# First pass of a two-layer attention kernel: turns and checks moved into the next step, products of qkv placed elsewhere in the step

## The chip, the cores and the metric

The kernel runs on one core of a Trainium2 chip. The metric is the device time of one execution in microseconds (us). Three runs of the kernel before gave a median of 4059.47 us (4054.06 to 4061.17). One execution was taken by the hardware profiler; it took 4056.18 us, with a span of 4054.4 us from the first to the last instruction. TensorE's granted clock was 0.992 over it.

The profile names the engines PE (TensorE matmul), PEld (TensorE's weight loads), DVE (VectorE), ACT (ScalarE), POOL (GpSimd) and SP (SyncE, which issues the DMAs here). L774 is line 774 of the kernel. An f32 matmul of 128x512 shows as two records, so "x8" in a row of the timeline is four matmuls.

## The reference

Two layers on an image batch of shape (8, 256, 64, 64), all in f32. Only layer 0 and the first product of layer 1 matter here; the rest is named.

```python
# layer 0: attention whose keys and values come from a 4x4 strided convolution
xr = conv(x, w_sr, stride 4); xr = layernorm over channels(xr) * g + b      # 16x16 places
q = w_q @ x;  k, v = split(w_kv @ xr)                                       # 8 heads of 32
attn = softmax(q k^T / sqrt(32))                                            # 4096 x 256 per head
x = x + gamma_s * (w_out @ (attn v))
# layer 1
qkv = w_qkv @ x                                                             # 768 x 4096 per image
agg = grouped 1x1 of depthwise 5x5 of qkv
x = x + batchnorm(w_proj @ relu_linear_attention(concat(qkv, agg)))
```

## The kernel before, in words

There are three passes, one after the other. The first does layer 0 and the product qkv of layer 1, and leaves its results in DRAM scratch (`planes`, `kd`, `vd`, `x2d`). The second does the convolution and the sums of layer 1, the third its output. Then a flag `fine`, made from checks in the first pass, says whether a general version must run instead; it does not run with these inputs. Only `first_pass` is touched.

**The loop of the first pass.** Its unit is a step n, one element of `order`: image b (8), strip s of 512 pixels (8), half c of the heads (2), half kc of the keys (2), so 256 steps, and some more at the end for what is left. A step n with kc = 1 is odd. In each step the code asks for, in this order:

- `scores` (L774): four matmuls, one head each, in four strips of 32 rows of TensorE, each into a bank of its own; then four Exp on ScalarE (L780) into tiles `e`.
- `valued` of the step before (L791): four matmuls into the tile `av`, in four strips of 32 columns.
- after both halves of the keys: `counted` (L807), the softmax sums `den`, from tiles `e` that `joined` (L802) has added on GpSimd; and `normed`, which divides. `normed` turns `den` on VectorE (L817), takes reciprocals of 16 columns (L818), turns them back (L820) and multiplies (L822). Two ScalarE activations of 128x512 (L823, L824) add up `den` and the reciprocals into `seen`, for the flag.
- `queries` (L759), the next q, in even steps.
- the work that `todo` holds for this step: `outputs` (`added`, L831 and L832: the product o with `w_out`, added to x, stored by L835), `differences` (L847 to L850), and products of `qkv`. The code asks for these last in the step, just ahead of the next step's scores.
- in some steps of an image, pieces of the next image's `keys_values` (sr at L687, mean, var, rs, k, v).

**The product qkv.** `w_qkv @ x` is done for a pair of row blocks and two strips by seven products in place of eight (`p1`, `p2`, `p6`, `p7`, `p4`, `p5`, `p3`). The sums of differences `t1` to `t4` and of weights `s1` to `s4` stand in for the eighth. Each product is one matmul of 128x512 (L875) into a bank; p1 is copied out by ScalarE (L925), the others are added on VectorE to an earlier part: L932, L936, L945 for the intermediate parts, `ended` for the outputs. For the outputs of pair 0, `ended` adds straight into a padded tile `stage` (L888). For pairs 1 and 2 it adds into `part_whole` (L891) and turns that with VectorE's 32x32 transpose into `turned` (L894); for pair 1 ScalarE also copies it into `stage` (L893). `stored` sends `stage` (L902) and `turned` (L912 for keys, L917 for values) to DRAM through SP's queue. `new_stage` clears two edges of a stage tile on GpSimd (L855, L856). A unit is done for every two strips, so in a cycle of 8 steps there are 21 products.

**Buffers.** `bank` gives one of five PSUM banks, tag "mm", to scores, q, o, qkv and the small products of the keys; a bank is used again when its reader is done. `av`, `den` and `sr` have banks of their own. `part_whole` has two buffers, each `stage` of pairs 0 and 1 one of its own (four tags), the tiles `e` twelve.

**What sets the order.** A scheduler builds each engine's stream from the code's order and the data. It can move instructions that are ready early. `tc.keep_in_program_order` pins an instruction behind all that its engine has been given so far. Each engine then takes its own stream in order; SP's DMA issues are one such stream.

Of the kernel before, what the change touches and what calls it, by code (L numbers as in the profile page):

```python
# [27 lines left out]
F32 = mybir.dt.float32  # L28
AF = mybir.ActivationFunctionType
ALU = mybir.AluOpType  # L30
AX = mybir.AxisListType

P = 128
# [541 lines left out]
def first_pass(ctx: ExitStack, tc: tile.TileContext, a, fine, planes, x2d, kd, vd, wtd):  # L575
# [207 lines left out]

    sums = {}

    def valued(b, s, c, kc, es):
        if kc == 0:
            sums["av"] = psum_early.tile([P, QB], F32, tag="av", name=f"av_{b}_{s}_{c}")
        for h in range(4):
            cols = slice(h * D0, (h + 1) * D0)  # L790
            nc.tensor.matmul(  # L791
                sums["av"][cols],
                vvs[b][:, kc, c * P + h * D0 : c * P + (h + 1) * D0],
                es[h],
                start=(kc == 0),
                stop=(kc == 1),
            )
# [11 lines left out]
    def normed(b, s, c):  # L809
        av, den = sums["av"], sums["den"]  # L810
        i = 2 * ((b * NG + s) * 2 + c)
        att = rest.tile([P, QB], F32, tag="att", name=f"att_{b}_{s}_{c}", bufs=4)
        r = rest.tile([P, NB, D0], F32, tag="rden", name=f"rden_{b}_{s}_{c}", bufs=1)
        one = two.tile([P, NB], F32, tag="one", name=f"one_{b}_{s}_{c}")
        nc.scalar.copy(att, av)

        nc.vector.transpose(r.rearrange("p n d -> p (n d)"), den)  # L817
        nc.vector.reciprocal(one, r[:, :, 0])  # L818
        r = rest.tile([P, NB, D0], F32, tag="rall", name=f"rall_{b}_{s}_{c}", bufs=1)
        nc.vector.transpose(r, one.unsqueeze(2).to_broadcast([P, NB, D0]))  # L820
        r = r.rearrange("p n d -> p (n d)")
        nc.vector.tensor_mul(att, att, r)  # L822
        nc.scalar.activation(den, den, AF.Copy, accum_out=seen[:, i : i + 1])  # L823
        nc.scalar.activation(den, r, AF.Copy, accum_out=seen[:, i + 1 : i + 2])  # L824
        return att

    def added(b, s, att, oc):
# [23 lines left out]
        quarters[b, g] = b11, b21, b22, t1, t2, t3, t4  # L851

    def new_stage(b, g, j):
        st = rest.tile([P, 4, NB + 1, NB + 1], F32, tag=f"stage{j}", name=f"stage_{b}_{g}_{j}", bufs=1)
        nc.gpsimd.memset(st[:, :, 0 if g // 2 else NB], 0.0)  # L855
        nc.gpsimd.memset(st[:, :, :, 0 if g % 2 else NB], 0.0)  # L856
        return st


    def qkv(b, g, pair):  # L860
        js = 2 * pair, 2 * pair + 1
        b11, b21, b22, t1, t2, t3, t4 = quarters[b, g]
        w = consts["wqkv"].rearrange("p c (j r o) -> p c j r o", j=3, r=2)[:, :, pair]
        s1, s2, s3, s4 = (combined[:, pair, i] for i in range(4))
        name = f"{b}_{g}_{pair}"
        stages = [new_stage(b, g, j) for j in js] if pair < 2 else None
        turned = None
        if pair:
            turned = [
                rest.tile([P, NB // 2, 4, D0], F32, tag=f"turned{j}", name=f"turned_{b}_{g}_{j}", bufs=1) for j in js  # L870
            ]

        def product(i, w, x):
            ps = bank(f"qkv_{name}_{i}")
            nc.tensor.matmul(ps, w, x, start=True, stop=True)  # L875
            return ps

        def part(i, bufs=1):
            return halves.tile([P, QB], F32, tag=f"part{i}", name=f"part_{name}_{i}", bufs=bufs)


        def ended(r, h, u, ps, op=ALU.add):
            if stages:
                y, x = g // 2, g % 2
                inside = stages[r][:, 2 * h : 2 * h + 2, y : y + NB, x : x + NB]
            rows = lambda t: t.rearrange("p (f y x) -> p f y x", f=2, y=NB)
            if not turned:
                nc.vector.tensor_tensor(inside, rows(u), rows(ps), op)  # L888
                return
            whole = part("whole", 2)  # L890
            nc.vector.tensor_tensor(whole, u, ps, op)  # L891
            if stages:
                nc.scalar.copy(inside, rows(whole))  # L893
            nc.vector.transpose(  # L894
                turned[r][:, :, 2 * h : 2 * h + 2].rearrange("p y f e -> p f y e"),
                whole.rearrange("p (f y e) -> p f y e", f=2, y=NB // 2),
            )

        def stored(r):
            j = js[r]  # L900
            if stages:
                nc.sync.dma_start(  # L902
                    planes[b, j].rearrange("g (k i f) e -> g k i (f e)", k=4, i=D1)[:, g],
                    stages[r].rearrange("p f y x -> p (f y x)"),
                )
            if not turned:
                return
            for k in range(4):
                n, src = 4 * (j % 2) + k, turned[r][k * D0 : (k + 1) * D0].rearrange("p y f e -> p y (f e)")
                if j < 4:  # L910
                    dst = kd[b][n].rearrange("a (y w) x b e -> a b (w x) y e", w=2)
                    nc.sync.dma_start(dst[g // 2, g % 2], src)  # L912
                else:
                    dst = vd[b][n][1 : NB2 + 1, 1 : NB2 + 1]
                    dst = dst.rearrange("(y w a) (x b) e -> a b w x y e", w=2, a=2, b=2)
                    for w in range(2):
                        nc.sync.dma_start(dst[g // 2, g % 2, w], src[w * NB : (w + 1) * NB])  # L917


        u = {}  # L920

        def p1():
            ps = product(1, w[:, 0, 0], b11)
            u[1] = part(1)
            nc.scalar.copy(u[1], ps)  # L925

        def p2():
            ended(0, 0, u[1], product(2, w[:, 1, 0], b21))

        def p6():  # L930
            u[2] = part(2)
            nc.vector.tensor_add(u[2], u[1], product(6, s2, t2))  # L932

        def p7():
            u[3] = part(3)
            nc.vector.tensor_add(u[3], u[2], product(7, s3, t3))  # L936

        def p4():
            ended(1, 0, u[3], product(4, w[:, 1, 1], t4), ALU.subtract)

        def p5():
            ps = product(5, s1, t1)
            ended(1, 1, u[3], ps)
            u[4] = part(4)
            nc.vector.tensor_add(u[4], u[2], ps)  # L945
            stored(1)

        def p3():
            ended(0, 1, u[4], product(3, s4, b22))
            stored(0)  # L950

        return [p1, p2, p6, p7, p4, p5, p3]

# [16 lines left out]
    q, es, att = {0: first}, {}, {}  # L970
    ahead = iter(())

    def outputs(b, s):
        return [lambda oc=oc: added(b, s, [att[b, s, 0], att[b, s, 1]], oc) for oc in range(2)]

    def qkv_lazy(b, g, pair):
        made = []

# [9 lines left out]

    n_all = len(order)
    todo = {}  # L990
    for n in range(n_all + 14):
        m = n - 1
        if n < n_all:
            b, s, c, kc = order[n]
            es[n] = scores(b, s, c, kc, q[n // 2])
        if 0 <= m < n_all:
            valued(*order[m], es[m])
            if order[m][3] == 1:
                counted(*order[m][:3], es.pop(m - 1))
                es.pop(m)  # L1000
                att[order[m][:3]] = normed(*order[m][:3])
        if n < n_all and kc == 1:
            joined(es[n - 1], es[n])
        if n < n_all and kc == 0 and n + 2 < n_all:
            q.pop(n // 2 - 1, None)
            q[n // 2 + 1] = queries(*order[n + 2][:3])
        if n >= 6 and (n - 6) % 8 == 4 and (n - 6) // 4 < B * NG:

            b, s = (n - 6) // 4 // NG, (n - 6) // 4 % NG
            work = [outputs(b, s) + [lambda b=b, s=s: differences(b, s // 2)]]  # L1010
            products = [p for pair in (1, 2, 0) for p in qkv_lazy(b, s // 2, pair)]
            for i in (4, 3, 4, 0, 3, 4, 3):
                work.append(products[:i])
                products = products[i:]
            for i, w in enumerate(work):
                todo.setdefault(n + i, []).extend(w)
        elif n >= 6 and (n - 6) % 8 == 0 and (n - 6) // 4 < B * NG:
            todo.setdefault(n, []).extend(outputs((n - 6) // 4 // NG, (n - 6) // 4 % NG))
        next(weights, None)
        if n < n_all:  # L1020
            b, at = n // 32, n % 32
# [2 lines left out]
            if b + 1 < B:  # L1024
# [6 lines left out]
                    next(ahead)  # L1031
                elif at >= 20:
                    next(ahead, None)
        for f in todo.pop(n, ()):
            f()
    for _ in weights:
        pass

# [3 lines left out]
    total = bank("total")[:, :2]  # L1042
    nc.tensor.matmul(total, mean_w, both, start=True, stop=True)
    fits = const.tile([P, 4], F32, tag="fits", name="fits")
    nc.vector.tensor_scalar(fits[:, 0:1], total[:, 0:1], SUM_MAX / C, None, ALU.is_le)
    nc.vector.tensor_scalar(fits[:, 1:2], total[:, 1:2], INVERSE_MAX / C, None, ALU.is_le)
    nc.vector.tensor_mul(fits[:, 2:3], fits[:, 0:1], fits[:, 1:2])
    nc.vector.tensor_copy(fine, fits[:, 2:3])

# [674 lines left out]
```

## Time and profile before

| | |
|---|---|
| median of 3 runs | 4059.47 us (4054.06 to 4061.17) |
| the profiled execution | 4056.18 us, span 4054.4 us |
| TensorE matmul busy | 3982.1 us |
| VectorE busy | 2262.4 us |
| ScalarE busy | 1644.2 us |
| GpSimd busy | 1275.1 us |
| first scores, and end of the first pass on TensorE | 52.42 us and 2154.75 us |
| turns L894, mean of one | 0.706 us |
| sums of products L891, mean of one | 0.67 us |
| stage copies L893, mean of one | 0.62 us |
| checks L823 and L824, mean of one, with the read of the sum | 0.582 + 0.194 and 0.602 + 0.186 us |
| GpSimd sums L802, mean of one | 1.320 us |

How to read it: a busy time is the time in which an instruction of the engine was under way, and for TensorE this includes time in which one of several matmuls in flight waits for its bank. Start-to-start distances in the timeline show such waits better than lengths do, since matmuls overlap by about 0.15 us. A row of the waits has the waiting line, the line waited for, the total in us, the number of times and the longest.

### The profile page before, as it was taken

To read this page: it belongs to the slowest core of one execution; us is meant where nothing else is said; L and a number is where in the kernel's file an instruction comes from. 1 tells how busy PE (TensorE), PEld (TensorE's weight loads), DVE (VectorE), ACT (ScalarE), POOL (GpSimd) and SP (SyncE) were. 2 spreads that over 40 slices of the span, in tenths; PEclk is the share of its full clock that TensorE was granted. 3 is DMA by queue.
4 is the path that set the end of the run, shared out by engine and by line. 5 is a ranking of instruction groups with operands and counts; after the bars stand their busy time and mean duration, and the time that the engine had idled before them with its cause. 6 is when DMAs were issued, how large, how long until landed. Compare 5 with 4: busy or idle time off the path is not lost. (4 is left out here: it accounts for less than half of the span.)

```text
span 4054.4 us, 70276 instructions
## 1 busy us (share of the span) xinstructions
PE 3982.1 (98%) x27074; PEld 2318.8 (57%) x27074; DVE 2262.4 (56%) x3752; ACT 1644.2 (41%) x3473; POOL 1275.1 (31%) x1394
## 2 busy tenths in 40 slices
PE   8999999999999999999998999999999998999999
PEld 4443434434334344343336888888888886556655
DVE  2676465564654545546565566666666664444443
ACT  3345354453544544534552222222222223454444
POOL 2344233333342433323343334434444441000000
PEclk9999999999999999999999999999999999999999
DMA  7665435445354354543549878778778656767674
GB/s 237 191 187 161 120 92 144 100 95 155 91 145 101 97 136 106 135 108 99 141 99 247 243 224 234 219 225 233 219 221 234 206 169 172 232 199 232 196 235 137
DMA packets 569898, 691.37 MB, mean 171 GB/s; under 512 B 60113, under 2 KB 429265, under 8 KB 565329
## 3 DMA queue, kind: packets, MB, share of 16 engines
q1 hardware_dynamic: 569552, 686.78, 60.6%
q8 instruction: 215, 3.52, 0.4%
q14 instruction: 131, 1.07, 0.1%
HBM read 412.54 MB, written 274.10 MB: 169 GB/s over the span
## 5 line engine op out<-in xcount | busy, mean ns | idle before, releaser
L802 POOL TENSOR_TENSOR e<-e,e 128x512 f32<-128x512 f32 x512 | 659.6, 1320 | 933.6 <-PE av L791 918.6
L780 ACT ACTIVATE e<-sc 128x512 f32<-128x512 f32 x1024 | 532.7, 601 | 708.8 <-PE sc L774 708.6
L774 PE MATMUL sc<-q,kk 32*128 32x512 f32 x2048 | 418.2, 641 | 7.5 <-ACT e L780 3.6
L1180 PE MATMUL cv<-w,c 128*128 128x128 f32 x3072 | 385.8, 280 | 6.0 <-POOL c L1124 6.0
L1180 PEld LDWEIGHTS cv<-w,c 128*128 128x128 f32 x3072 | 359.9, 193 | 35.5 <-issue 28.8
L1547 DVE TENSOR_TENSOR y<-z,xs 128x256 f32<-128x256 f32 x256 | 143.7, 648 | 312.8 <-ACT z L1538 305.2
L1222 PE MATMUL sums<-vq,r 128*32 128x288 f32 x4096 | 307.4, 413 | 0.0
L891 DVE TENSOR_TENSOR part_whole<-part,qkv 128x512 f32<-128x512 f32 x256 | 170.7, 670 | 219.6 <-PE qkv L875 215.8
L774 PEld LDWEIGHTS sc<-q,kk 32*128 32x128 f32 x2048 | 130.0, 183 | 276.3 <-issue 138.3
L1196 ACT ACTIVATE r<-s 128x512 f32<-128x512 f32 x256 | 160.5, 627 | 294.0 <-DVE s L1195 290.9
L875 PE MATMUL qkv<-differences,combined 128*128 128x512 f32 x576 | 278.7, 593 | 0.8 <-DVE differences L848 0.8
L791 PE MATMUL av<-e,vv 128*32 128x512 f32 x2048 | 275.6, 608 | 0.0
L1538 ACT ACTIVATE z<-p,bn 128x256 f32<-128x256 f32 x256 | 133.7, 578 | 315.9 <-PE p L1529 208.7
L759 PE MATMUL q<-x,wq 128*128 128x512 f32 x512 | 254.4, 619 | 0.0
L1184 PE MATMUL cv<-c,w 128*128 128x128 f32 x2048 | 253.4, 278 | 0.0
L1529 PE MATMUL p<-att,wproj 128*128 128x512 f32 x512 | 249.5, 610 | 1.9 <-ACT att L1512 1.9
L1187 ACT COPY both<-cv 128x512 f32<-128x512 f32 x128 | 74.9, 585 | 432.4 <-PE cv L1180 374.1
L687 PE MATMUL sr<-x,wsr 128*128 128x256 f32 x1024 | 237.2, 386 | 11.5 <-DMA wsr<-in_w_sr_dram 11.5
L1529 PE MATMUL p<-agg,wproj 128*128 128x512 f32 x512 | 241.7, 595 | 0.0
L1184 PEld LDWEIGHTS cv<-c,w 128*128 128x128 f32 x2048 | 239.7, 192 | 0.0
L687 PEld LDWEIGHTS sr<-x,wsr 128*128 128x128 f32 x1024 | 193.3, 192 | 76.3 <-issue 32.8
L831 PE MATMUL o<-att,wout 128*128 128x512 f32 x512 | 231.9, 594 | 0.0
(143 smaller groups left out, 6201.7 us busy)
## 6 DMA issues: line engine op xcount, KB each, us to landing
vq<-v SPq DMA_DIRECT2D x256, 384.0 KB
planes<-stage SPq DMA_DIRECT2D x128, 578.0 KB
d<-planes SPq DMA_DIRECT2D x128, 578.0 KB
raw<-planes SPq DMA_DIRECT2D x128, 272.0 KB
x<-in_xp_dram SPq DMA_DIRECT2D x64, 512.0 KB
wsr<-in_w_sr_dram SPq DMA_DIRECT2D x128, 256.0 KB
x<-x SPq DMA_DIRECT2D x128, 256.0 KB
k<-turned SPq DMA_DIRECT2D x256, 128.0 KB
```

Source lines behind the costliest of these rows:

```text
L687: nc.tensor.matmul(ps[:, oc], w[:, ci, oc * P : (oc + 1) * P], xt[:, ci, f * NK : (f + 1) * NK], start=(f == ci == oc == 0), stop=(f == R ...
L759: nc.tensor.matmul(ps, consts["wq"][:, ci, c * P : (c + 1) * P], x_tiles[b][:, ci, s * QB : (s + 1) * QB], start=(ci == 0), stop=(ci == 1),)
L774: nc.tensor.matmul(scs[h], kks[b][rows, c, kc * P : (kc + 1) * P], qs[rows], start=True, stop=True)
L780: nc.scalar.activation(e, scs[h], AF.Exp, scale=D0**-0.5)
L791: nc.tensor.matmul(sums["av"][cols], vvs[b][:, kc, c * P + h * D0 : c * P + (h + 1) * D0], es[h], start=(kc == 0), stop=(kc == 1),)
L802: nc.gpsimd.tensor_tensor(es0[h], es0[h], es1[h], ALU.add)
L831: nc.tensor.matmul(ps, consts["wout"][:, c, oc * P : (oc + 1) * P], att[c], start=(c == 0), stop=(c == 1))
L875: nc.tensor.matmul(ps, w, x, start=True, stop=True)
L1180: nc.tensor.matmul(out, x, m, start=(da == 0), stop=(da == 1))
L1184: nc.tensor.matmul(out, m, x, start=(da == 0), stop=(da == 1))
L1222: nc.tensor.matmul(ps[h * D0 : (h + 1) * D0, : 36 * D1].rearrange("p (r n e) -> p r n e", r=3, e=D1), kt[:, par, h, 2 * r + c], vq[:, r : ...
L1529: nc.tensor.matmul(ps.rearrange("p (f q n) -> p f q n", f=4, q=4), wproj[:, j, oc * P : (oc + 1) * P], src, start=(j == 0), stop=(j == 3),)
```

## The change

There are five edits, all in `first_pass`.

1. A list `late` holds functions that are to run in the next step, right after that step's scores. `ended` puts its turn and its stage copy there (both pinned in program order), for pairs 1 and 2; `ready` puts `stored` of these pairs there. `part_whole` becomes `whole`, with six buffers.
2. `normed` no longer reads 128x512 twice for the checks. It puts `noted` into `late`: two ScalarE copies of 128x16, of the first column of each turned block and of the reciprocals, with the same sums into `seen`. The limits in the flag are divided by 32 to fit.
3. The step's order changes. In odd steps the qkv products of that step come right after scores, ahead of `valued`. In even steps they come after `valued` and ahead of `queries`. `queries` comes ahead of `counted` and `normed`.
4. `added` runs within the step, after `joined`, in every fourth step as before; the 21 products are spread as 2, 3, 4, 1, 4, 3, 4 over the seven steps after it, where it was 4, 3, 4, 0, 3, 4, 3.
5. `stage` of pairs 0 and 1 share their buffers (two tags in place of four).

```diff
     def normed(b, s, c):
...
-        nc.scalar.activation(den, den, AF.Copy, accum_out=seen[:, i : i + 1])
-        nc.scalar.activation(den, r, AF.Copy, accum_out=seen[:, i + 1 : i + 2])
+
+        def noted():
+            for k, t in enumerate((turn[:, :, 0], one)):
+                copy = two.tile([P, NB], F32, tag="copy", name=f"copy_{b}_{s}_{c}_{k}")
+                tc.keep_in_program_order(
+                    nc.scalar.activation(copy, t, AF.Copy, accum_out=seen[:, i + k : i + k + 1])
+                )
+
+        late.append(noted)
...
     def new_stage(b, g, j):
-        st = rest.tile([P, 4, NB + 1, NB + 1], F32, tag=f"stage{j}", name=f"stage_{b}_{g}_{j}", bufs=1)
+        st = rest.tile([P, 4, NB + 1, NB + 1], F32, tag=f"stage{j % 2}", name=f"stage_{b}_{g}_{j}", bufs=1)
...
         def ended(r, h, u, ps, op=ALU.add):
...
-            whole = part("whole", 2)
+            whole = halves.tile([P, QB], F32, tag="whole", name=f"whole_{name}_{r}_{h}", bufs=6)
             nc.vector.tensor_tensor(whole, u, ps, op)
-            if stages:
-                nc.scalar.copy(inside, rows(whole))
-            nc.vector.transpose(
-                turned[r][:, :, 2 * h : 2 * h + 2].rearrange("p y f e -> p f y e"),
-                whole.rearrange("p (f y e) -> p f y e", f=2, y=NB // 2),
-            )
+
+            def turn():
+                tc.keep_in_program_order(
+                    nc.vector.transpose(
+                        turned[r][:, :, 2 * h : 2 * h + 2].rearrange("p y f e -> p f y e"),
+                        whole.rearrange("p (f y e) -> p f y e", f=2, y=NB // 2),
+                    )
+                )
+                if stages:
+                    tc.keep_in_program_order(nc.scalar.copy(inside, rows(whole)))
+
+            late.append(turn)
...
+        def ready(r):
+            if turned:
+                late.append(lambda: stored(r))
+            else:
+                stored(r)
...
-    for n in range(n_all + 14):
+    for n in range(n_all + 16):
         m = n - 1
         if n < n_all:
             b, s, c, kc = order[n]
             es[n] = scores(b, s, c, kc, q[n // 2])
+        was, late[:] = list(late), []
+        for f in was:
+            f()
+
+
+        if n % 2:
+            for f in todo.pop(n, ()):
+                f()
         if 0 <= m < n_all:
             valued(*order[m], es[m])
-            if order[m][3] == 1:
-                counted(*order[m][:3], es.pop(m - 1))
-                es.pop(m)
-                att[order[m][:3]] = normed(*order[m][:3])
-        if n < n_all and kc == 1:
-            joined(es[n - 1], es[n])
+        for f in todo.pop(n, ()):
+            f()
         if n < n_all and kc == 0 and n + 2 < n_all:
             q.pop(n // 2 - 1, None)
             q[n // 2 + 1] = queries(*order[n + 2][:3])
-        if n >= 6 and (n - 6) % 8 == 4 and (n - 6) // 4 < B * NG:
-
+        if 0 <= m < n_all and order[m][3] == 1:
+            counted(*order[m][:3], es.pop(m - 1))
+            es.pop(m)
+            att[order[m][:3]] = normed(*order[m][:3])
+        if n < n_all and kc == 1:
+            joined(es[n - 1], es[n])
+        if n >= 6 and (n - 6) % 4 == 0 and (n - 6) // 4 < B * NG:
             b, s = (n - 6) // 4 // NG, (n - 6) // 4 % NG
-            work = [outputs(b, s) + [lambda b=b, s=s: differences(b, s // 2)]]
-            products = [p for pair in (1, 2, 0) for p in qkv_lazy(b, s // 2, pair)]
-            for i in (4, 3, 4, 0, 3, 4, 3):
-                work.append(products[:i])
-                products = products[i:]
-            for i, w in enumerate(work):
-                todo.setdefault(n + i, []).extend(w)
-        elif n >= 6 and (n - 6) % 8 == 0 and (n - 6) // 4 < B * NG:
-            todo.setdefault(n, []).extend(outputs((n - 6) // 4 // NG, (n - 6) // 4 % NG))
+            for oc in range(2):
+                added(b, s, [att[b, s, 0], att[b, s, 1]], oc)
+            if s % 2:
+                differences(b, s // 2)
+                products = [p for pair in (1, 2, 0) for p in qkv_lazy(b, s // 2, pair)]
+                for i, count in enumerate((2, 3, 4, 1, 4, 3, 4)):
+                    todo[n + 1 + i] = products[:count]
+                    products = products[count:]
...
-        for f in todo.pop(n, ()):
-            f()
...
-    nc.vector.tensor_scalar(fits[:, 0:1], total[:, 0:1], SUM_MAX / C, None, ALU.is_le)
-    nc.vector.tensor_scalar(fits[:, 1:2], total[:, 1:2], INVERSE_MAX / C, None, ALU.is_le)
+    nc.vector.tensor_scalar(fits[:, 0:1], total[:, 0:1], SUM_MAX / D0 / C, None, ALU.is_le)
+    nc.vector.tensor_scalar(fits[:, 1:2], total[:, 1:2], INVERSE_MAX / D0 / C, None, ALU.is_le)
```

More of the change, by code (lines that the diff above doesn't have):

```diff
@@ L784, in first_pass @@
     sums = {}
+    late = []
     def valued(b, s, c, kc, es):
@@ L812, in normed @@
         att = rest.tile([P, QB], F32, tag="att", name=f"att_{b}_{s}_{c}", bufs=4)
-        r = rest.tile([P, NB, D0], F32, tag="rden", name=f"rden_{b}_{s}_{c}", bufs=1)
+        turn = rest.tile([P, NB, D0], F32, tag="rden", name=f"rden_{b}_{s}_{c}", bufs=1)
         one = two.tile([P, NB], F32, tag="one", name=f"one_{b}_{s}_{c}")
         nc.scalar.copy(att, av)
-        nc.vector.transpose(r.rearrange("p n d -> p (n d)"), den)
-        nc.vector.reciprocal(one, r[:, :, 0])
+        nc.vector.transpose(turn.rearrange("p n d -> p (n d)"), den)
+        nc.vector.reciprocal(one, turn[:, :, 0])
         r = rest.tile([P, NB, D0], F32, tag="rall", name=f"rall_{b}_{s}_{c}", bufs=1)
@@ L876, in product, with part @@
             return ps
-        def part(i, bufs=1):
-            return halves.tile([P, QB], F32, tag=f"part{i}", name=f"part_{name}_{i}", bufs=bufs)
+        def part(i):
+            return halves.tile([P, QB], F32, tag=f"part{i}", name=f"part_{name}_{i}", bufs=1)
         def ended(r, h, u, ps, op=ALU.add):
@@ L945, in p5 @@
             nc.vector.tensor_add(u[4], u[2], ps)
-            stored(1)
+            ready(1)
         def p3():
             ended(0, 1, u[4], product(3, s4, b22))
-            stored(0)
+            ready(0)
         return [p1, p2, p6, p7, p4, p5, p3]
@@ L971, in first_pass @@
     ahead = iter(())
-    def outputs(b, s):
-        return [lambda oc=oc: added(b, s, [att[b, s, 0], att[b, s, 1]], oc) for oc in range(2)]
     def qkv_lazy(b, g, pair):
```

## The prediction

> **What bounds the kernel now.** I read the page first, then TensorE's timeline, then the table of waits from 500 to 2100 us. Only the first pass is changed; its TensorE work runs to 2154.75 us of the 4054.4 us span, and passes two and three stay as they are.
>
> ```profile
> PE 3982.1 (98%) x27074; PEld 2318.8 (57%) x27074; DVE 2262.4 (56%) x3752; ACT 1644.2 (41%) x3473; POOL 1275.1 (31%) x1394
> L802 POOL TENSOR_TENSOR e<-e,e 128x512 f32<-128x512 f32 x512 | 659.6, 1320 | 933.6 <-PE av L791 918.6
> ```
>
> TensorE looks full, so the only thing to win is time in which it is counted busy while it waits. The timeline shows that time. Columns: start, length, engine, line, tile, count.
>
> ```profile
> 866.16 1.14 PE L774 MATMUL sc<-q,kk 32*128 32x512 f32 x8
> 867.23 1.07 PE L791 MATMUL av<-e,vv 128*32 128x512 f32 x8
> 868.23 1.99 PE L875 MATMUL qkv<-x,wqkv 128*128 128x512 f32 x4
> 870.05 1.88 PE L875 MATMUL qkv<-differences,combined 128*128 128x512 f32 x4
> 871.86 1.64 PE L774 MATMUL sc<-q,kk 32*128 32x512 f32 x8
> 873.43 1.07 PE L791 MATMUL av<-e,vv 128*32 128x512 f32 x8
> 874.32 1.04 PE L807 MATMUL den<-e,ones_w 128*32 128x512 f32 x8
> 875.29 1.99 PE L759 MATMUL q<-x,wq 128*128 128x512 f32 x4
> 877.11 1.02 PE L875 MATMUL qkv<-differences,wqkv 128*128 128x512 f32 x2
> 877.97 1.02 PE L875 MATMUL qkv<-differences,combined 128*128 128x512 f32 x2
> 878.83 1.02 PE L875 MATMUL qkv<-x,combined 128*128 128x512 f32 x2
> 879.78 2.17 PE L774 MATMUL sc<-q,kk 32*128 32x512 f32 x8
> 881.88 1.06 PE L791 MATMUL av<-e,vv 128*32 128x512 f32 x8
> ```
>
> From the start of the four scores to the start of av it is 1.07 us at 866.16 (after the o products), but 1.57 at 871.86 and 2.10 at 879.78, both straight after qkv products. The scores need four of five banks "mm", which the products have just filled. What they wait for:
>
> ```profile
> PEld sc L774 <- DVE part L945: 39.1, 68, 0.7
> PEld sc L774 <- ACT stage L893: 37.1, 49, 0.8
> PEld sc L774 <- DVE part L932: 12.0, 50, 0.4
> PEld sc L774 <- DVE part_whole L891: 12.0, 12, 1.3
> ```
>
> These are the evictions of the last products, held back on VectorE by the turns (L894, 0.71 us each) and on ScalarE by the stage copies (L893, 0.62). I took the cycle of 8 steps from 866.16 to 923.10, 56.94 us, in which no keys are made: scores lose 3.6 us over 1.07 each. So waiting is about 6% of the pass.
>
> **What the Trainium skill says.** "TensorEngine Tiling (Array Packing)", Key Properties: changing the tiling mode drains TensorE. The trace agrees in kind: one matmul 128x512 follows another after 0.86 us, but av to a 128*128 product takes 1.00, that first product 0.96, and the last product before scores 0.95. The same page, Gotcha 1: PSUM Pressure, says that row tiles write to different banks; the four scores do. "TensorE: Matmul & The Clock Gate", Architectural detail: ScalarE and VectorE queues are strict FIFO; that an eviction stands behind a turn, as L932 behind L894 here, fits.
>
> **The change part by part,** from the built order of instructions on each engine, with n the step.
> - Turns, stage copies and their stores go into the next step, behind its exps. Counts stay: 256 turns, 128 copies, the same DMAs. Priced at nothing on TensorE if the product's own eviction now runs ahead; checked below.
> - Small checks: per head group two 128x512 activations with sum reads go (0.58+0.19+0.60+0.19 = 1.56 us, 128 times, 200 us of ScalarE), two 128x16 copies with reads come. The nearest row, 128x36 at 0.19, plus 0.19 gives 256 x 0.38 = 97 us. ScalarE is idle over half of the pass, so neither is on the path; in the step where they stand ahead of a product's eviction I count 0.4 us, as these small ones overlap. If that cover went, 0.4 us in one step of 8, 13 us in all.
> - Order on TensorE: odd steps become scores, products, av; even ones scores, av, products, q, den, o. Products per step from n = 3 (mod 8): 2, 3, 4, 1, 4, 3, 4, 0; before 4, 3, 4, 0, 3, 4, 3, 0.
> - Pairs 0 and 1 share two stage buffers, so POOL's memsets wait for the store of the other pair. Stores land 4 to 5 us after issue (issued at 1028.14, the memset released at 1033.38); by the order the memset's next user stands over 15 us after the step that issues it. Priced at nothing; if late, the POOL sums queued behind it are late, and den behind them.
> - SP: the k stores now stand ahead of the planes stores, and two wsr loads behind stores of a later step; the built order has also moved their products back, behind the first o of the next step. Such a load is issued by about 7.8 us after the odd step's scores (the last stage sum ends at 6.15, two stores and the load take 0.53 each), its product comes at 5.71 + 7.9 = 13.6: 5 us to land 256 KB, where stores of 578 KB take 4 to 5. Priced at nothing; without that cover sr would wait, some 1 us per image.
>
> **The prices not shown.** Scores to a 128*128 product is shown once:
>
> ```profile
> 52.42 1.14 PE L774 MATMUL sc<-q,kk 32*128 32x512 f32 x8
> 53.50 1.98 PE L759 MATMUL q<-x,wq 128*128 128x512 f32 x4
> 55.41 1.41 PE L774 MATMUL sc<-q,kk 32*128 32x512 f32 x8
> ```
>
> 1.08 us. Product to av or to den isn't shown: I take 0.09 as product to scores; bounds 0 and 0.22 (scores to av over the 0.85 of av itself). There are 251 of them: -23 to +33 us. den to scores: 0.97 as den to q; bounds 0.88 and 1.07.
>
> **Step by step, no waits.** Odd with 4 products: 1.08 + 0.96 + 3x0.86 + 0.09 + av 1.00 = 5.71. With 2: 3.99. Even with 3: 1.07 + 1.00 + 0.96 + 2x0.86 + q 1.81 + den 0.97 = 7.53. With o and none: 1.07 + 1.00 + 1.91 + 0.97 + o 3.63 = 8.58; with o and one: 9.44. The cycle is 3x5.71 + 3.99 + 2x7.53 + 8.58 + 9.44 = 54.20. Before, 56.94 - 3.6 = 53.3: the switches of mode take 0.9 of the 3.6 back.
>
> **What is late next.** Banks: in a step of 4 products VectorE works the sums of the step before until 2.7 us after the scores, a turn to 3.4, then the evictions; the last of those that the next scores need ends at 5.45, and the scores start at 5.71. No wait, by 0.26 us. In the step of 2 products the first product waits for the second o to be added (0.3 us). den: POOL's four sums start 1.19 us after av and take 4.96:
>
> ```profile
> 1024.21 1.07 PE L791 MATMUL av<-e,vv 128*32 128x512 f32 x8
> 1025.41 5.41 POOL L802 TENSOR_TENSOR e<-e,e 128x512 f32<-128x512 f32 x4 [12.28 <-PE av L791]
> ```
>
> av now stands behind the products, so the sums end 6.15 us after a later av; den starts 1.00 + 1.07 + 1.00 + 1.91 = 4.98 after it where no product follows: a wait of 1.15. With one product, 0.3. With three, none. Behind the waiting den stand o and then the next scores. Cycle: 54.20 + 0.3 + 1.15 + 0.3 = 55.95, a gain of 1.0 us.
>
> **The sum.** Cycles with keys (923.10 to 1005.05, 1005.05 to 1072.05): sr and the like now stand behind av or den alone, 0.19 more per step for about 4 steps, less 0.3 of the den wait: gain 0.5. Per image 2x1.0 + 2x0.5 = 3.0; eight images, the last without keys: 25. The first 115 us have den waiting for POOL by 4.32, 2.49, 4.01, 4.04 and 0.90 us; q in front of den covers up to 1.91 each: 8.5. Together 33 us, of the profiled execution's own 4056.2: 4023. The median of the runs is 3.3 above that execution: **4026 us**.
>
> **Rivals.**
> 1. *den becomes the bound (slower).* Place: POOL sums behind a later av. If they end L later than I count, den loses 2L more per cycle, above 1.4 us in all four even steps. The gain of 1.0 is gone at L = 0.5. For: some sums take 5.4 us instead of 4.96, and an av behind products also waits on their banks. Against: with sr in the odd step there is no wait. L = 1 loses 2.0 per cycle, over 32 cycles 64: 4026 + 64 = 4090.
> 2. *The banks still wait (no change).* The cover is 0.26 us in three steps of 8. VectorE late by 0.6 takes 0.34 each, 1.0 per cycle: 4057. For: 2.7 us of sums and a turn stand in front. Against: before, these gave 2.10 with no product between.
> 3. *Better than counted.* Switches of mode free and no den wait: 33 + 32x0.9 + 32x1.45 = 108 less: 3951; half of that surplus, 3988.
> 4. *Nothing moves,* the scheduler restoring the old order: excluded by the built order, which differs.
>
> **How the numbers follow.** A measurement here tells apart about 0.2%, 8 us. The forecast case (3990 to 4051) has 0.52, rival 3 below that 0.13, rival 2 0.14, rival 1 0.21. Faster by over 0.2% is 0.65, within 0.14, slower 0.21. The range is 3985 to 4080, from the half surplus to most of rival 1; the unknown switches (-23 to +33) lie in it.
>
> **What would show it.** Right: scores to av or to a product about 1.08 in nearly all steps; the waits of sc on DVE part and ACT stage gone; den waiting for POOL e by about 1.1 us in steps without products; cycle without keys near 56.0; L823's and L824's 1.56 us gone from ScalarE. Wrong: scores at 1.5 or more after odd steps (rival 2), den waiting 2 us or in steps with three products (rival 1), POOL's memset waiting on planes for long with the sums behind it, or a product to av well above 0.95.

## The result, and the profile after

The changed kernel takes **4038.27 us** (4035.43 to 4043.45), beside 4057.05 for the kernel before on the same chip: ratio 0.9954, 95% interval 0.9940 to 0.9969. The forecast was 4026, with a range of 3985 to 4080 and faster as the likeliest side. That is 18.8 us less where 33 were counted.

The profiled execution took 4043.45 us (span 4041.7), 5.2 above the median; that of before took 4056.18. Two lines of its page:

```profile
PE 3954.6 (98%) x27074; PEld 2260.2 (56%) x27074; DVE 2250.5 (56%) x3752; ACT 1511.8 (37%) x3473; POOL 1275.2 (32%) x1394
L774 PE MATMUL sc<-q,kk 32*128 32x512 f32 x2048 | 312.9, 642 | 11.7 <-DVE x L841 5.3
```

ScalarE is busy for 132 us less. The scores' busy time fell from 418.2 to 312.9 us: waits for banks were inside it, as a group of four scores is drawn out when one of the four comes late. TensorE's timeline of a cycle without keys shows where they went (start, length, engine, line, tile, count):

```profile
904.24 1.14 PE L774 MATMUL sc<-q,kk 32*128 32x512 f32 x8
905.32 1.12 PE L885 MATMUL qkv<-differences,combined 128*128 128x512 f32 x2
906.28 1.02 PE L885 MATMUL qkv<-differences,wqkv 128*128 128x512 f32 x2
907.13 1.02 PE L885 MATMUL qkv<-differences,combined 128*128 128x512 f32 x2
907.99 1.02 PE L885 MATMUL qkv<-x,combined 128*128 128x512 f32 x2
908.95 1.07 PE L793 MATMUL av<-e,vv 128*32 128x512 f32 x8
909.94 1.14 PE L774 MATMUL sc<-q,kk 32*128 32x512 f32 x8
911.01 1.06 PE L793 MATMUL av<-e,vv 128*32 128x512 f32 x8
912.01 1.98 PE L759 MATMUL q<-x,wq 128*128 128x512 f32 x4
913.92 1.06 PE L809 MATMUL den<-e,ones_w 128*32 128x512 f32 x6
915.14 1.04 PE L809 MATMUL den<-e,ones_w 128*32 128x512 f32 x2 [0.16 <-POOL e L804]
```

From scores to product it is 1.08 us, from scores to av 1.07 (909.94 to 911.01), where it was up to 2.10. In exchange den's last quarter starts 1.22 us after den's start: it waits for POOL's fourth sum. The table of waits from 500 to 2100 us has that wait, and none of the scores (sc) for a stage or for a part on VectorE:

```profile
PEld den L809 <- POOL e L804: 47.5, 64, 1.1
```

The cycle without keys, from the scores after one o to those eight steps later (863.72 to 919.75), takes 56.03 us; 55.95 was predicted and 56.94 was measured before. The cycle is as computed, and yet the total isn't. Reading each image by the start of the o products of its last block shows why. Here and in the second such table, the first three columns are us against the same event, or the same length, in the kernel before; the last column is the time itself, from the last o to the second pass's first group of 48 cv matmuls (its convolution), which waits for that pass's first load behind the stores.

| kernel | end of image 1 | each of images 2 to 7 | last o | last o to the 48 cv |
|---|---|---|---|---|
| before | 0 (at 337.1) | 0 (263.0 long) | 0 (at 2131.0) | 40.6 |
| changed | +8.7 | -5.8 | -27.3 | 54.1 |

These are single executions, and the changed kernel's was the longest of its five, so a few us of the first image may be of the execution. The first image became longer; images 2 to 7 each became shorter by nearly twice what was counted; image 8, which has no keys to make, gained 1.4 us; and 13.5 us are given back where the first pass ends.

### The profile page after: what moved, and what is told of

Same layout as the page of the kernel before. It is cut to its first block, busy times and chain, and to the rows that moved or that the text cites. A ratio compares the mean times of both kernels' runs of the same rounds, so it can differ in the third digit from the quotient of the medians.

```text
span 4041.7 us, 70298 instructions
## 1 busy us (share of the span) xinstructions
PE 3954.6 (98%) x27074; PEld 2260.2 (56%) x27074; DVE 2250.5 (56%) x3752; ACT 1511.8 (37%) x3473; POOL 1275.2 (32%) x1394
## 5 line engine op out<-in xcount | busy, mean ns | idle before, releaser
L1205 PEld LDWEIGHTS cv<-w,c 128*128 128x128 f32 x3072 | 361.1, 193 | 40.6 <-issue 30.3
L774 PE MATMUL sc<-q,kk 32*128 32x512 f32 x2048 | 312.9, 642 | 11.7 <-DVE x L841 5.3
L885 PE MATMUL qkv<-differences,combined 128*128 128x512 f32 x576 | 306.4, 623 | 1.9 <-DVE whole L901 1.0
L819 DVE STREAM_TRANSPOSE rden<-den 128x512 f32<-128x512 f32 x128 | 91.7, 716 | 369.6 <-PE den L809 369.5
L759 PE MATMUL q<-x,wq 128*128 128x512 f32 x512 | 245.3, 601 | 0.2 <-DVE whole L901 0.2
L1220 DVE TENSOR_TENSOR s<-cv,both 128x512 f32<-128x512 f32 x256 | 172.1, 673 | 87.6 <-PE cv L1209 43.5
```

The costliest lines, as they stand in the source:

```text
L759: nc.tensor.matmul(ps, consts["wq"][:, ci, c * P : (c + 1) * P], x_tiles[b][:, ci, s * QB : (s + 1) * QB], start=(ci == 0), stop=(ci == 1),)
L774: nc.tensor.matmul(scs[h], kks[b][rows, c, kc * P : (kc + 1) * P], qs[rows], start=True, stop=True)
L1205: nc.tensor.matmul(out, x, m, start=(da == 0), stop=(da == 1))
```

## The experiments

Unless said otherwise, an edit is against the changed kernel; times are medians, ratios are to the kernel before.

**Theory A:** putting off the turns and stage copies is what frees the banks. **Rivals:** the order of the steps does, or the small checks.

**1. Turns put off, in the old order (e2_turns).** This kernel also shares the stages, as the changed kernel does. Edit of the kernel before:

```
-        st = rest.tile(..., tag=f"stage{j}", bufs=1)
+        st = rest.tile(..., tag=f"stage{j % 2}", bufs=1)
...
-            whole = part("whole", 2)
+            whole = halves.tile(..., tag="whole", bufs=6)
...
+            def turn(): ...          # transpose, stage copy
+            late.append(turn)        # run behind the next step's exps
```

> The kernel before with one part of the change alone: the turns, stage copies and stores are put off to the step that follows (six buffers for whole, stages shared by two); the order on TensorE, the products of each step and the large checks of the sums stay as before. Theory A, the putting off is what frees the banks, and the new order only costs it (switches of mode, and den waiting for the sums): the scores after qkv products start some 0.3 to 0.6 us later than 1.07 instead of 0.5 to 1.03, no wait of den in the steady part; the cycle without keys goes from 56.94 to about 55.0, 1.9 for each of 32 cycles, about 60 us less: 3997. Theory B, a product has to be followed by something other than scores for the banks to come free, and putting off alone moves a wait onto the next instruction of VectorE: cycle 56.5 or more, within 0.3% of 4057.

4055.01 us, ratio 0.9990 (0.9982 to 0.9998): Theory A's 60 us did not come. TensorE's timeline in two steps of this kernel:

```profile
872.00 1.14 PE L774 MATMUL sc<-q,kk 32*128 32x512 f32 x8
873.07 1.06 PE L793 MATMUL av<-e,vv 128*32 128x512 f32 x8
873.96 1.55 PE L809 MATMUL den<-e,ones_w 128*32 128x512 f32 x8
875.43 1.98 PE L759 MATMUL q<-x,wq 128*128 128x512 f32 x4
...
879.92 1.71 PE L774 MATMUL sc<-q,kk 32*128 32x512 f32 x8
881.56 1.06 PE L793 MATMUL av<-e,vv 128*32 128x512 f32 x8
```

The scores at 872.00, after four products, no longer wait (1.07 to av, 1.57 before); those of another such step of the cycle still take 1.46. Those after three products still take 1.64 (2.10 before), as p5's bank is read by two VectorE additions in a row, and a den of 1.04 us became one of 1.55: part of the time that scores no longer wait, den does. The cycle from 866.30 to 922.43 takes 56.13, later ones 55.91, so some banks do come free sooner. At its last o the kernel is 15.3 us ahead, and 12.2 of these are lost on the way to the second pass (52.8 us). Experiment 7 shows what the shared stages have to do with that.

**2. The order and small checks, turns at once (e3_order).**

```
-            late.append(turn)
+            nc.vector.transpose(...)
+            nc.scalar.copy(inside, rows(whole))
```

> The changed kernel with its new order on TensorE and its small checks, but the turns, stage copies and stores at once, as before. Theory A (the putting off frees the banks): the evictions of a step of four products again stand behind turns, but av of 1.00 us now stands between the last product and the scores; sc waits about 0.2 to 0.6 in three odd steps of 8, POOL's sums end later, so the cycle without keys is about 56.5 to 57.5 and the time 4040 to 4075. Theory B (av between products and scores is what removes the wait): as the changed kernel, 4038 within 5.

4037.65 us, ratio 0.9947 (0.9934 to 0.9959), the same as the changed kernel, and its cycle is the same 56.03. For the new order Theory A falls: behind av, an eviction that stands after a turn is still early enough. In the two profiled executions a later image is 0.6 us shorter with the putting off and the first 5.8 longer (+8.7, +2.9 without); the medians, 0.6 us apart, say that it is worth nothing in all in this order.

**3. The large checks put back (e4_checks).**

```
-            late.append(noted)       # two 128x16 activations, in the next step
+        nc.scalar.activation(den, den, AF.Copy, accum_out=...)
+        nc.scalar.activation(den, r, AF.Copy, accum_out=...)
```

> The changed kernel with the large checks back: two 128x512 activations with sum reads on ScalarE for each head group instead of two 128x16 ones in the next step. Theory A (ScalarE is off the path): 4038 within 6, with ScalarE busy 120 to 140 us more. Theory B (ScalarE's time before the exps or before the q eviction counts): 0.6 us or more in half of the even steps, 4055 or more.

4055.94 us, ratio 0.9997 (0.9989 to 1.0005): some 17.7 us, nearly all that the change brings, hang on the small checks. (They are smaller and also stand a step later; the two weren't tried apart.) The cycle takes 57.07. TensorE's timeline in the step that corresponds to the one above:

```profile
906.23 1.13 PE L879 MATMUL qkv<-differences,combined 128*128 128x512 f32 x2
907.41 1.13 PE L879 MATMUL qkv<-differences,wqkv 128*128 128x512 f32 x2
908.51 1.13 PE L879 MATMUL qkv<-differences,combined 128*128 128x512 f32 x2
909.47 1.02 PE L879 MATMUL qkv<-x,combined 128*128 128x512 f32 x2
910.42 1.07 PE L793 MATMUL av<-e,vv 128*32 128x512 f32 x8
```

The second and third product come 1.18 and 1.10 us after the one ahead, not 0.96 and 0.85; from the first product to av it is 4.19 instead of 3.63. ScalarE's timeline tells what they wait for:

```profile
906.19 0.58 ACT L826 ACTIVATE den<-den 128x512 f32<-128x512 f32 x1 [1.33 <-DVE rden L819]
906.68 0.19 ACT L826 ACTIVATION_READ_ACCUMULATOR den<-den 128x1 f32 x1
906.77 0.59 ACT L780 ACTIVATE e<-sc 128x512 f32<-128x512 f32 x1
907.25 0.60 ACT L827 ACTIVATE den<-rall 128x512 f32<-128x512 f32 x1
907.77 0.20 ACT L827 ACTIVATION_READ_ACCUMULATOR den<-rall 128x1 f32 x1
907.86 1.57 ACT L780 ACTIVATE e<-sc 128x512 f32<-128x512 f32 x3
```

The scores hold four of the five banks, so the second product needs the bank that the first exp frees (it ends at 907.36, the product starts at 907.41), and the third that of the second exp. The large activations stand before and between these exps. A cycle has two such steps, so about 1.1 us of waiting. In the changed kernel all four exps run at once, and the small ones follow:

```profile
905.46 2.07 ACT L780 ACTIVATE e<-sc 128x512 f32<-128x512 f32 x4 [1.52 <-PE sc L774]
```

**4. The small checks alone (e7_small), the kernel before with noted() only.** 

> The kernel before with the small checks alone, in the next step behind the exps; order, turns and stages as before. Theory E (ScalarE's large activations cost only where products stand directly behind the scores and need a bank that the exps free): before, av stands there and den's activations run under o and products, so about 0 to 5 us less, 4053 to 4058. Rival F (they hold ScalarE ahead of evictions that the scores wait for, whatever the order): 15 to 20 us less, 4040.

4057.87 us, ratio 1.0003 (0.9995 to 1.0012): nothing, and its cycle, 56.97, is that of before. In the old order av stands behind every scores, and needs no bank that these exps free.

**5. The order alone (e8_order), with turns at once, large checks and stages as before.** 

> The new order alone: turns and stores at once, stages as before, large checks. Theory E: the order gains 31 us up to the last scores with small checks, and loses 0.55 us in two of the four-product steps of a cycle with the large ones (measured with turns put off), 14 to 18 us in all; nothing is given back at the end of the pass as the stages aren't shared: 4040 to 4048. Rival F (small checks are worth the same in any order, and the order gains all by itself only with turns put off): 4052 or more.

4044.92 us, ratio 0.9971 (0.9963 to 0.9980), 12.7 us less. Its cycle without keys takes 57.15, longer than before; its gain lies in the two cycles with keys of an image (80.62 and 65.71, where 81.95 and 67.00 were). With experiments 3, 4 and 6 this settles the parts: the order is worth 12.7 us by itself, and the small checks 0 in the old order and 14 to 18 in the new one (14.4 between this kernel and that of experiment 6). The gain of the cycle that the prediction worked out needs both. The pieces of the order (where products stand, how many in each step, q ahead of den) were not taken apart.

**6. Stage buffers not shared (e6_stages).** Edit of experiment 2's kernel:

```
-        st = rest.tile(..., tag=f"stage{j % 2}", bufs=1)
+        st = rest.tile(..., tag=f"stage{j}", bufs=1)
...
-            whole = halves.tile(..., tag="whole", bufs=6)
+            whole = halves.tile(..., tag="whole", bufs=2)
```

> The run of the new order with turns at once (4037.65) once more, but pairs 0 and 1 have stage buffers of their own again, as before; to make room for them, whole has its two buffers again. Theory C (what is given back where the first pass ends comes from the shared stages: the last pair's sums into its stages wait for the stores of the pair before, so the last stores and the first load of the second pass behind them on SP are late): from the sums' product total to the third group of cv products 17 us instead of 26.3, and about 9 us less, 4029. Rival D (the second pass waits for its loads in any case, longer when the first pass ends earlier): 26 us stay, 4038 within 5.

4030.56 us, ratio 0.9936 (0.9923 to 0.9949), 7 less than experiment 2 by the medians, though the intervals overlap. From the last o to the 48 cv it is 41.1 us; it was 50.3. ScalarE's timeline of experiment 2 (shared) in the last unit of work, then that of this kernel:

```profile
2121.86 2.17 ACT L908 COPY stage<-whole 128x512 f32<-128x512 f32 x4
```

```profile
2111.68 0.62 ACT L908 COPY stage<-whole 128x512 f32<-128x512 f32 x1 [2.92 <-DVE whole L901]
...
2118.30 0.62 ACT L908 COPY stage<-whole 128x512 f32<-128x512 f32 x1 [1.04 <-DVE whole L901]
```

With shared buffers the built order on ScalarE has all four stage copies of the last unit behind later work, though the last `whole` that they read was ready by 2116.5. SP's queue is next, of the shared kernel and then of this one:

```profile
2123.05 0.52 SPq L913 DMA_DIRECT2D planes<-stage  x1
...
2142.77 1.77 SPq L1110 DMA_DIRECT2D d<-planes  x1
```

```profile
2116.37 0.52 SPq L913 DMA_DIRECT2D planes<-stage  x1
...
2135.93 1.75 SPq L1110 DMA_DIRECT2D d<-planes  x1
```

In both, 19.6 to 19.7 us, filled with stores, lie between the first planes store of the last unit and the second pass's first load; only the start differs. With stages of their own the last o comes at 2103.6, with shared ones at 2101.4, so against the last o the start is 8.9 us earlier.

**7. Sharing alone (e10_shared), the same line in the kernel before.** 

> The kernel before with one line changed: pairs 0 and 1 share the two stage buffers. Theory C (sharing costs at the end of the first pass, whatever the order): the steps stay as they are, and from the sums' product total to the third group of cv products it takes some 25 us instead of 16.9: 8 us slower, 4066. Rival: the loss at the end needs the new order or put-off stores: 4058 within 4.

4065.82 us, ratio 1.0019 (1.0012 to 1.0027), 8.0 slower, with the images unchanged (last o +0.6) and 50.6 us to the 48 cv instead of 40.6. The profiled execution is the shortest of the 17 (4059.96 us): at the 48 cv it is 10.6 us behind, and it ends only 3.8 behind, so the 8.0 us rest on the runs, and the trace shows only where they start. The loss at the end is that of the shared stages, whatever the order. Why the built order places the copies so is not shown; that both the copies and the stores after them are late is.

This changes how experiment 1 reads. It shares the stages too, and has a ratio of 0.9990 where sharing alone has 1.0019: in the old order the putting off brings some 0.3%, or 11 us (each ratio is against the kernel before on its own chip), and the shared stages take most of it back.

**8. One sum on VectorE (e5_den).**

```
-            nc.gpsimd.tensor_tensor(es0[h], es0[h], es1[h], ALU.add)
+            e = nc.vector if n % 4 == 1 and h == 3 else nc.gpsimd
+            e.tensor_tensor(es0[h], es0[h], es1[h], ALU.add)
```

> The changed kernel with the fourth of POOL's four sums of exps given to VectorE, in steps whose number is 1 (mod 4), which are those that an o step without or with one product follows. Theory A (den waits for POOL's sums alone, 1.23 and 0.38 us a cycle): the waits of den on POOL e go, the cycle without keys falls from 56.03 to about 54.5, 30 to 45 us less over the pass: 3995 to 4010. Theory B (VectorE is too full, so its sum comes late, or the evictions behind it do): den waits on VectorE instead or sc does, 4030 to 4045.

4021.75 us, ratio 0.9906 (0.9891 to 0.9921); the cycle is 54.88. den's wait of 1.2 us falls to 0.43, that of 0.38 to none. The total stays above what was expected for two reasons: the first image is 4.1 us longer still (+12.8 instead of +8.7), and a later image gains only 2.9 us more, where 1.15 in each of its four cycles would be 4.6.

**9. The parts that pay, together (e9_best): experiment 6 and 8.** 

> What seems best of all so far: new order, small checks, turns and stores at once, stages not shared, and the fourth sum of exps on VectorE in the steps whose number is 1 (mod 4). If the gains add up (16 of the sum, 9 of the stages): 4012 to 4016. If turns at once and the sum collide on VectorE, the scores wait for banks again: 4020 or more.

4004.61 us, ratio 0.9872 (0.9858 to 0.9887). Against experiment 6 that is 26 us, some 9 more than the sum brought in experiment 8. In the traces most of this is the first image, which is 1.3 us longer than before here, with turns at once, and not 12.8.

**10. A second sum on VectorE (e11_sums), where n is 1 (mod 8).** 

> The best kernel so far (4004.6), and in the steps whose number is 1 (mod 8) VectorE also takes the third sum of exps. den still waits 0.43 us there, once in a cycle of 8 steps: if POOL's sums are what is left, 0.43 for each of 32 cycles, 10 to 14 us less, 3991 to 3995. If VectorE's additional 0.6 us makes evictions late, 4003 or more.

4001.86 us, ratio 0.9864 (0.9849 to 0.9879); the two intervals overlap, so the 2.8 us are not shown by the times. In the trace the cycle goes from 54.9 to 54.5 and the last o is 10.8 us earlier, but that execution (3993.91) was the shortest of its four, 8 us below the median.

**11. The weight products moved out of the first image (e12_spread).** What was left was the first image. In the changed kernel VectorE's timeline there has L663, one of 32 products wb of the second pass's weights, ahead of the additions that evict, and TensorE's shows the scores that wait:

```profile
321.11 1.75 DVE L663 TENSOR_TENSOR wb<-wd,wsmall 128x1536 f32<-128x1536 f32 x1
322.78 0.68 DVE L901 TENSOR_TENSOR whole<-part,qkv 128x512 f32<-128x512 f32 x1
323.38 0.68 DVE L967 TENSOR_TENSOR part<-part,qkv 128x512 f32<-128x512 f32 x1
```

```profile
321.92 1.13 PE L774 MATMUL sc<-q,kk 32*128 32x512 f32 x6
324.11 1.12 PE L774 MATMUL sc<-q,kk 32*128 32x512 f32 x2 [1.06 <-DVE part L967]
```

A product also holds VectorE longer than it runs. All 32 of the kernel before, then of the changed kernel (busy, mean of one in ns, idle before):

```profile
L663 DVE TENSOR_TENSOR wb<-wd,wsmall 128x1536 f32<-128x1536 f32 x32 | 61.1, 1910 | 36.2 <-DMA wt<-wb 36.1
L663 DVE TENSOR_TENSOR wb<-wd,wsmall 128x1536 f32<-128x1536 f32 x32 | 61.9, 1933 | 53.9 <-DMA wt<-wb 53.8
```

`wb` has one buffer, so VectorE stands still ahead of a product until the store of the one before has read it, with the evictions behind it in its stream. The edit:

```
-                nc.vector.tensor_tensor(
+                made_w = nc.vector.tensor_tensor(
...
+                tc.keep_in_program_order(made_w)
...
-        next(weights, None)
+        if n % 4 == 0:
+            next(weights, None)
```

> The changed kernel with one thing moved: the 32 products of the second pass's weights on VectorE (L663, 128x1536, 1.85 us each), which it does one a step in the first image, are spread over the eight images, one in each fourth step behind the q product, in program order. Theory G (these stand ahead of evictions in the first image, where banks are tighter in the new order, and that is why the first image became 8.7 us longer instead of shorter): by the last o of the first image it is at least 10 us earlier than the changed kernel was, later images lose 0 to 1 us each: 4022 to 4034. Rival H (the first image's loss is den waiting for the sums or the first loads): 4036 or more.

4020.34 us, ratio 0.9907 (0.9894 to 0.9921). The 32 products now lie in the first four images, not in all eight as the text above has it. VectorE stands idle ahead of them for 0.1 us in all. At the end of image 1 it is 28.5 us ahead of before, where the changed kernel was 8.7 behind: 37.2 us for some 23 products that are gone from there. Images 2 to 4, with about eight products each, gain only 0.8 us each, and images 5 to 7 their full 5.8. A product of 1.8 us costs some 0.6 us of the pass there, and more than twice that in the first image. That they are spread and that they are kept in order was not tried apart, and the kernel before was not run with its products spread, though they stand in its first image too.

**12. The same on the best kernel (e13_spread).** 

> The same on the best kernel so far (two sums on VectorE, turns at once, stages not shared, 4001.86). Theory G: the first image 5 to 10 us shorter, the others 0 to 1 us longer: 3990 to 4000. If VectorE, with its sums, has no room for them in the later images: 4004 or more.

**3979.78 us**, ratio 0.9805 (0.9791 to 0.9818), faster than both kernels: new order, small checks, turns at once, stages not shared, two sums on VectorE, weight products spread. The first image ends 33.2 us earlier than before, images 5 to 7 take 9.0 less each, and the last o comes at -79.6. That is more than expected in the first image; images 2 to 4, which now hold the products, gain 4.1 each, where they gained 8.5 in experiment 10.

The end of image 1, the later images and the way to the second pass, of the kernels that separate the parts (the number of the experiment in brackets):

| kernel | end of image 1 | each of images 2 to 7 | last o | last o to the 48 cv |
|---|---|---|---|---|
| turns put off, stages shared (1) | +8.3 | -3.3 | -15.3 | 52.8 |
| order, small checks (2) | +2.9 | -5.2 | -29.7 | 50.3 |
| changed, large checks (3) | +3.6 | -3.1 | -12.8 | 53.9 |
| order alone (5) | -0.2 | -2.3 | -11.6 | 41.2 |
| order, small checks, own stages (6) | +5.4 | -5.2 | -27.4 | 41.1 |
| changed, one sum moved (8) | +12.8 | -8.7 | -45.3 | 54.3 |
| 6 and 8 (9) | +1.3 | -7.6 | -49.6 | 41.5 |

## Why the prediction was right, and where it was not

**Right:** that waits for banks are in the busy time of the scores, that they go, and what comes in their place. The cycle was right to 0.08 us, and so were nearly all of its terms: product to av 0.95 us with the counted switch of 0.09; den to scores 0.99 (0.97 counted); den's waits 1.23 and 0.38 (1.15 and 0.3). The wait of the first product for x was 0.12 instead of 0.3. Rival 2 fell: no score of that cycle waits for more than 0.1 us. Rival 1 fell too: the sums came late by 0.08, where 0.5 would have taken the gain.

**The sum was near by luck.** Four terms of it failed, with both signs:

- *The cycles with keys, "gain 0.5" each.* They went from 81.95 to 80.63 and from 67.00 to 64.56, gains of 1.3 and 2.4. I took over the cycle without keys and subtracted switches. In the trace of before, the 16 scores of these two cycles lose 8.2 us over 1.07 each, and 0.3 after, and only one den of theirs waits, for 1.2. So a later image gains 5.8 us, not 3.0: 16.7 more over images 2 to 7. Image 8, which has only cycles without keys, was counted with 4.0 and brought 1.4.
- *The first 115 us, "8.5".* By the second o it was 2.0, and by the end of the first image 8.7 were lost. I looked only at den there, and not at who else is on VectorE in the first image. With the 3.0 that any image was to gain, this step is off by some 20 us. Experiment 11 shows that L663 costs some 37 us of the first image in the new order. Why the image became longer than in the kernel before, which has the same products in it, stays open: VectorE's idle time ahead of L663 does not follow the loss (47.2 us and -0.2 at the end of image 1 with the order alone, 33.0 and +8.3 with the turns put off).
- *Shared stages, "priced at nothing".* I followed the memsets inside the pass, where nothing depends on them, and not the end of it, where the store chain stands ahead of the next pass's load. Measured alone: 8.0 us (experiment 7), and 9.1 in the trace with the new order (50.3 to 41.1). Of the 13.5 us that are given back there in the changed kernel, 3.8 more are of the putting off (54.1 with it, 50.3 without), by which the last unit's copies and stores stand a step later, and 0.6 are left for the order.
- *Small checks, "neither is on the path".* True of the kernel before (experiment 4), false of the order into which they go: products now stand directly behind the scores and take the banks that the exps free. They are worth 14 to 18 us there: without them the cycle is 57.07 and not 56.03, and its whole gain is gone. I named their cover, and priced its loss at 13 us "in the step where they stand ahead of a product's eviction"; the place was another one, the exps. As the change brings both together, the forecast wasn't hurt, but its account of what does the work was: the putting off of the turns, to which its check of the banks was given, does nothing measurable in the new order.

At the last o 27.3 us were gained, against 33 counted: 20 too few in the first image, 17 too many in images 2 to 7, 3 too few in image 8. That these nearly cancel is luck. After the 13.5 given back, 13.8 remain at the 48 cv. The profiled executions differ by 12.7 and the medians by 18.8, as that of the changed kernel is 5.2 above its median and that of before 0.9 below.

## What to carry to other kernels

Look at who frees a buffer for whatever will stand next in the new order, not in the old: work that is hidden today can be on the path tomorrow, and the other way round. Price a steady cycle, but then walk the first and the last round on each engine and each queue on their own; two of the four errors here, and a gain of 22 us (by moving set-up work out of the first round), were there. A buffer that is shared to make room has to be priced where its last user ends, with what stands behind that store.

## What the runs showed of the hardware

- A wait for a bank hardly shows as idle time of TensorE here. Before, only 7.5 us of idle time stood ahead of the scores, and yet their busy time fell by 105 us (418.2 to 312.9), while one matmul took the same (641 and 642 ns). The four of a group run side by side, and with one of them late the group is drawn out. The start-to-start distance shows it.
- An activation of 128x16 with a sum read took 0.23 to 0.25 + 0.22 us; both of a head group lie within 0.54 us (907.39 to 907.93), since the parts overlap. The saving against two of 128x512 is 132 us of ScalarE, 103 were counted.
- A change of the tile form costs little and evenly: a product behind av or scores takes 0.96 instead of 0.86, a product to av 0.95, av to a product 1.00 against 0.88 to den. This agrees with the drain that "TensorEngine Tiling (Array Packing)", Key Properties, names without a size.
